# Squares in the diagonal blocks of a graph-attention layer's second pass, and an even pace for its finished rows

## The chip, the cores and the metric

The kernel runs on one NeuronCore of a Trainium2 chip. Its engines work in parallel, each through its own instructions in order: TensorE (PE; its weight loads are listed as PEld), VectorE (DVE), ScalarE (ACT), GpSimd (POOL) and SyncE (SP), which here only issues DMA transfers. On-chip data lies in SBUF and, for matmul results, in PSUM. The metric is the device time of one execution in microseconds (us).

## The reference

The input is x, 4096 x 512, and a sparse 0/1 matrix adj, 4096 x 4096. There are two layers; the change is in the first.

```
# layer 0
h = relu(layernorm(x))
node_att = softmax(h @ node_w, axis=0)
g = h @ edge_w
e = where(adj > 0, g @ g.T, -9e15)
edge_att = softmax(e, axis=1)
x = x + (adj * node_att * edge_att) @ (h @ weight) + bias
# layer 1: attention of 8 heads on the new x
h = relu(layernorm(x))
d = (h @ W.T + b) as (4096, 8, 64)
e = leaky_relu(src(d)[n] + trg(d)[m], 0.01) + adj
x = x + softmax(e) @ d
```

The score matrix g @ g.T is symmetric. All is computed in 32-bit floats.

## The kernel before

Rows are handled in 32 tiles of P = 128, and in 8 blocks of BL = 512 (TB = 4 tiles).

*First pass over the scores.* The blocks (i, j) with j >= i are computed on TensorE, written to `e_d` in HBM, and used for the row maxima. Only the upper half of the scores is stored; in a diagonal block, tile t stores the columns from its own start on.

*Second pass* (lines 364 to 486, from 700 to 1601 us). The outer loop runs over the blocks b of 512 output rows, the inner one over the tiles m of 128 neighbours: 256 steps (b, m). A step needs the scores of its 128 neighbours against the block's 512 rows, with neighbours in the partitions. It subtracts the row maxima (L441) and adds the mask (`mk`, L435; the sum is L442), takes the exponential on ACT (`ex`, L444), multiplies by adj (`at`, L450), adds `ex` to a sum on POOL (`racc`, L460), and multiplies `at` with the tile's rows of `sup` = h @ weight on TensorE into four PSUM tiles `po` (L480). Each 32-bit matmul shows as two records.

Where the scores come from depends on m. For tiles above the block (m // TB < b) they are loaded as they are (`et`, L396). For tiles below it (m // TB > b) the stored scores lie the other way round. They are then loaded in squares of S = 32 that stand at their transposed places (`squares`, L402 to L411: 16 DMAs for a group of four tiles into one buffer `eb`), and DVE, whose transpose turns each square of 32 x 32 in itself, turns them into a PSUM tile `pt` (L421). In the diagonal block (m // TB == b) the group's four row tiles are loaded into one `eb` (L392); for its tile i the first i of four column parts are missing, and TensorE transposes them from the tiles before (L427), i = 1, 2 and 3, six transposes of 128 x 128 in a block.

*The order of the work* is written out by hand. The loop at L652 to L669 calls the stages of several steps in turn: `load` of the step 8 ahead, `squares` of that 9 ahead, `turn` 3 ahead, `exps` 2, `masks` 3, `weigh` (L450, L460) 1 ahead, then `gather` (L480) of the step itself. Every engine and every DMA queue runs its instructions in this order. The loads of the second pass go through SP's queue; buffers come free when DVE has used them (11 for `a`, the tile of adj, 9 for `et`, 4 for `eb`, 3 for `at`).

*Finishing rows.* At a block's last step ACT copies its four `po` tiles to SBUF. During the next block, after `weigh`, the loop calls `finish` (L490) once for each of the four row tiles: DVE scales by the node attention and adds x (L499), and POOL issues a DMA to `x1` (L500). This happens at steps m = 2, 3, 4, 5 while b < 3, and at 2, 4, 6, 8 from b = 3 on.

*The path to layer 1.* Row tiles in `SQ` (L511) get their layer norm at once: `finish` adds bn_stats (L505), `layernorm` (L514) follows from m = 10 on, and the normalised rows are written to `h_d` as squares (SP, L532). Rows outside `SQ`, those of the first and the last block, are normalised later. After the second pass the loop `tail` (L615 to L648, 1601 to 1717 us) takes one row tile a step: `fetch` (L550) loads it; `stats` and `norm` normalise it if it is not in `SQ`; `turn_h` (L574) transposes it, on DVE from squares if it is in `SQ` (L577), otherwise on TensorE with a copy on ACT (L583, L585); `linear` (L587, L591) multiplies by W. Layer 1's attention follows from 1720 us on.

Of the kernel before, what the change touches and what calls it, by code (L numbers as in the profile page):

```python
# [15 lines left out]
P = 128  # L16
# [12 lines left out]
def kernel(  # L29
# [15 lines left out]
    nc = tc.nc  # L45
# [6 lines left out]
    BL = 512  # L52
    NB = N // BL
    TB = BL // P
# [3 lines left out]
    ident = const.tile([P, P], FP, name="ident")  # L58
# [17 lines left out]
    S = 32  # L76
    e_d = dram.tile([N, N + 2 * S], FP, name="e_d")[:, 0:N]
# [23 lines left out]
    with tc.tile_pool(name="w0", bufs=1) as wp, tc.tile_pool(name="a0", bufs=2) as ap_, tc.tile_pool(  # L101
# [32 lines left out]
        def stats(t):  # L134
            st = sp.tile([P, 6], FP, name="st")
            nc.vector.bn_stats(st, xts[t])
            mvs[t] = sp.tile([P, 2], FP, name="mv")
            nc.vector.bn_aggr(mvs[t], st)
            sds[t] = sp.tile([P, 1], FP, name="sd")
            nc.scalar.activation(sds[t], mvs[t][:, 1:2], AF.Sqrt, bias=eps)  # L140

        def norm(t):
            rs = sp.tile([P, 1], FP, name="rs")
            nc.vector.reciprocal(rs, sds.pop(t))
            mr = sp.tile([P, 1], FP, name="mr")
            nc.vector.scalar_tensor_tensor(mr, mvs.pop(t)[:, 0:1], -1.0, rs, op0=ALU.mult, op1=ALU.mult)
            hs[t] = sp.tile([P, F], FP, name="h", bufs=5)
            if t < T0:
                nc.scalar.activation(hs[t], xts[t], AF.Relu, bias=mr, scale=rs)
            else:  # L150
                nc.scalar.activation(squares_of(hs[t]), columns_of(xts[t]), AF.Relu, bias=mr, scale=rs)
# [24 lines left out]
        def turn(t):  # L176
            b, j = divmod(t, TB)
            if j == 0:
                hts[b] = ap_.tile([P, KC, BL], FP, name="h_t")
            if t >= T0:  # L180
                nc.vector.transpose(
                    hts[b][:, :, j * P:(j + 1) * P].rearrange("p k (a q) -> p k a q", q=S),
                    hqs.pop(t).rearrange("p (a k q) -> p k a q", k=KC, q=S))
                return
            h = hs.pop(t)
            pt = pp.tile([P, KC, P], FP, name="pt")
            for k in range(KC):
                nc.tensor.transpose(pt[:, k, :], h[:, k * P:(k + 1) * P], ident)
            nc.vector.tensor_copy(hts[b][:, :, j * P:(j + 1) * P], pt)
            logit(t, h)  # L190
# [25 lines left out]
        def step(t):  # L216
            if t < NT:
                upto(fetch, t + 10 if t >= T0 else t + 7)
                upto(norm, t + 4)
                upto(send, t + 4)  # L220
                turn(t)
                upto(pull, t + 2)
                upto(stats, t + 5)
# [47 lines left out]
    def maxima(i, acc, psum, pool):  # L271

        mx = pool.tile([P, TB], FP, name="mx")
        nc.vector.tensor_reduce(mx, rm[:, i * TB:(i + 1) * TB, i:NB], AX.X, ALU.max)
        pc = psum.tile([P, TB, P], FP, name="pt")
        for j in range(TB):
            nc.tensor.transpose(pc[:, j, :], acc[:, j * P:(j + 1) * P], ident)
        cm = pool.tile([P, TB], FP, name="cm")
        nc.vector.tensor_reduce(cm, pc, AX.X, ALU.max)
        nc.vector.tensor_tensor(mx, mx, cm, ALU.max)  # L280
        yield
        pm = psum.tile([P, BL], FP, name="pt")
        nc.tensor.transpose(pm[:TB, 0:P], mx, ident)
        ms = pool.tile([TB, P], FP, name="ms")
        nc.vector.tensor_copy(ms, pm[:TB, 0:P])
        nc.gpsimd.dma_start(mx_d[i], ms)


    with tc.tile_pool(name="mx", bufs=1) as mxp, tc.tile_pool(name="b_a", bufs=6) as adjp, tc.tile_pool(
# [6 lines left out]
        loaded, masks = {}, {}  # L296
# [52 lines left out]
        for n in range(-6, len(items)):  # L349
# [3 lines left out]
            if n >= 0:  # L353
                i, j, t = items[n]
# [9 lines left out]
    with tc.tile_pool(name="c_a", bufs=11) as adjp, tc.tile_pool(name="c_b", bufs=4) as ebp, tc.tile_pool(  # L364
# [10 lines left out]
        src, pts, aj, mks, ex, at = {}, {}, {}, {}, {}, {}  # L375

        def rows_of(m):
            return slice(m * P, (m + 1) * P)
# [23 lines left out]
        def squares(b, m):  # L402
            cols = slice(b * BL, (b + 1) * BL)
            if m // TB > b and m % TB == 0:
                eb = ebp.tile([P, TB, BL], FP, name="eb")
                sq = e_d[cols, m * P:m * P + BL].rearrange("(a p) (i c q) -> i c p a q", p=S, q=S, i=TB)
                for i in range(TB):
                    for c in range(P // S):
                        nc.sync.dma_start(eb[c * S:(c + 1) * S, i, :].rearrange("p (a q) -> p a q", q=S), sq[i, c])
                for i in range(TB):  # L410
                    src[b, m + i] = eb  # L411

        def turn(b, m):

            i = m % TB
            eb = src[b, m]
            pt = p_t.tile([P, BL], FP, name="pt")
            pts[b, m] = pt
            parts = []
            if m // TB > b:  # L420
                nc.vector.transpose(pt, eb[:, i, :])  # L421
                src[b, m] = [(slice(0, BL), pt)]
                return
            n = i if m // TB == b else 0
            if n > 0:
                for j in range(n):
                    nc.tensor.transpose(pt[:, j * P:(j + 1) * P], eb[:, j, i * P:(i + 1) * P], ident)  # L427
                parts.append((slice(0, n * P), pt))
            if n < TB:
                parts.append((slice(n * P, BL), eb[:, i, :] if m // TB == b else eb))  # L430
            src[b, m] = parts
# [56 lines left out]
        left, scale, norms = [], {}, iter(())  # L488

        def finish():  # L490

            t, acc, oc, rs, xt = left.pop(0)
            b, j = divmod(t, TB)
            if j == 0:
                sc = sp.tile([P, TB], FP, name="sc")
                nc.vector.reciprocal(sc, rs)
                nc.vector.tensor_tensor(sc, sc, na[:, b * TB:(b + 1) * TB], ALU.mult)
                scale[b] = sc
            nc.vector.scalar_tensor_tensor(oc, acc, scale[b][:, j:j + 1], xt, op0=ALU.mult, op1=ALU.add)  # L499
            nc.gpsimd.dma_start(x1[rows_of(t), :], oc)  # L500
            if t in SQ:
                if j == 0:
                    mv4[b] = sp.tile([P, TB, 2], FP, name="mv4", bufs=1), []
                st = sp.tile([P, 6], FP, name="st", bufs=4)
                nc.vector.bn_stats(st, oc)  # L505
                nc.vector.bn_aggr(mv4[b][0][:, j, :], st)
                mv4[b][1].append(oc)

        SQ = range(TB, (NB - 1) * TB)  # L511
        mv4 = {}

        def layernorm(b):  # L514
# [35 lines left out]
        def fetch(t):  # L550
            xl[t] = etp.tile([P, BL], FP, name="et")
            nc.sync.dma_start(xl[t], h_d[t] if t in SQ else x1[rows_of(t), :])

        def stats(t):
            if t in SQ:
                return
# [7 lines left out]
        def norm(t):  # L564
            if t in SQ:
                return
# [7 lines left out]
        def turn_h(t):  # L574
            if t in SQ:
                hts[t] = wkp.tile([P, BL], FP, name="d")
                nc.vector.transpose(hts[t].rearrange("p (k a q) -> p k a q", k=KC, q=S),  # L577
                                    xl.pop(t).rearrange("p (a k q) -> p k a q", k=KC, q=S))
                return
            h = hs.pop(t)  # L580
            pt = p_t.tile([P, BL], FP, name="pt")
            for k in range(KC):
                nc.tensor.transpose(pt[:, k * P:(k + 1) * P], h[:, k * P:(k + 1) * P], ident)  # L583
            hts[t] = wkp.tile([P, BL], FP, name="d")
            nc.scalar.copy(hts[t], pt)  # L585
# [27 lines left out]
        end = len(steps)  # L613
# [35 lines left out]

        stages = ((load, 8), (squares, 9), (turn, 3), (exps, 2), (masks, 3), (weigh, 1), (gather, 0))  # L652
        for s in range(-9, end):
            for f, ahead in stages:
                if 0 <= s + ahead < end:
                    f(*steps[s + ahead])
                if f is weigh:
                    b, m = divmod(s, NT)
                    if left and m > 1 and (m % 2 == 0 or b < 3):
                        finish()  # L660
                    if m == 10 and b - 1 in mv4:
                        norms = layernorm(b - 1)
                    if m >= 10:
                        next(norms, None)
                    tail(s - end)
                    if s == 3:
                        ending = maxima(NB - 1, acc_z, p_t, sp)
                    if s in (3, 4):
                        next(ending, None)  # L669
# [10 lines left out]
        pt = p_t.tile([P, BL], FP, name="pt")  # L680
# [53 lines left out]
    with tc.tile_pool(name="p", bufs=2) as prp, tc.tile_pool(name="rl", bufs=2) as rlp, tc.tile_pool(  # L734
# [322 lines left out]
        stages = ((load, 4), (exps, 1), (weigh, 1), (factors, 2), (logs, 0), (scale, 2), (gather, 0))  # L1057
# [48 lines left out]
```

## Time and profile before

| | |
|---|---|
| median of 3 runs | 2953.14 us (2951.71 to 2954.64) |
| the profiled execution: its time, its span | 2952.01 us, 2949.9 us |
| TensorE busy over the span | 2895.0 us, 98% |
| DVE, ACT, POOL busy | 2535.0, 1318.9, 1421.7 us |
| second pass, first to last matmul of L480 | 705.6 to 1601.3 us |
| tail, first matmul of L591 to its end | 1604.1 to 1717.3 us |
| mean of one transpose: TensorE 128 x 128 (L427, 48 of them), DVE 128 x 512 (L421, 112) | 282 ns, 720 ns |

The span runs from the first instruction to the last; the execution's time also holds what lies around it, 2.1 us here. Engine times are busy times. A matmul's record is longer than its share of TensorE, as the next one starts before it ends, so distances between starts tell how long a step lasts. A group's row gives source line, engine, operation, the tiles written and read, their sizes and the count; then the busy time and the mean of one, and the idle time before it with what ended it. In a row of the timeline the start and the length in us come first, and in brackets stands how long the engine was idle before, and what released it.

### The profile page before, as it was taken

To read this page: it belongs to the slowest core of one execution; us is meant where nothing else is said; L and a number is where in the kernel's file an instruction comes from. 1 tells how busy PE (TensorE), PEld (TensorE's weight loads), DVE (VectorE), ACT (ScalarE), POOL (GpSimd) and SP (SyncE) were. 2 spreads that over 40 slices of the span, in tenths; PEclk is the share of its full clock that TensorE was granted. 3 is DMA by queue.
4 is the path that set the end of the run, shared out by engine and by line. 5 is a ranking of instruction groups with operands and counts; after the bars stand their busy time and mean duration, and the time that the engine had idled before them with its cause. 6 is when DMAs were issued, how large, how long until landed. Compare 5 with 4: busy or idle time off the path is not lost.

```text
span 2949.9 us, 42840 instructions
## 1 busy us (share of the span) xinstructions
PE 2895.0 (98%) x15051; PEld 1152.0 (39%) x15051; DVE 2535.0 (86%) x3584; ACT 1318.9 (45%) x1822; POOL 1421.7 (48%) x1075
## 2 busy tenths in 40 slices
PE   8999999999999999999999989999999999999998
PEld 4444444444444444444444423333233223232223
DVE  5535777778888998998996789999999999999998
ACT  2211111111121221222222068888777777777776
POOL 3401111113544444444444766676767676766675
PEclk9999999999999999999999989999999999999999
DMA  5525666667875766756644269898989898989796
GB/s 182 175 75 199 223 220 224 226 218 192 202 178 162 174 166 185 187 161 179 198 160 135 61 173 237 232 229 237 234 241 232 238 231 237 235 237 233 208 226 168
DMA packets 488616, 583.47 MB, mean 198 GB/s; under 512 B 265464, under 2 KB 315672, under 8 KB 488400
## 3 DMA queue, kind: packets, MB, share of 16 engines
q1 hardware_dynamic: 431920, 406.70, 45.2%
q0 software_dynamic: 54464, 170.10, 26.1%
q10 hardware_dynamic: 2016, 3.93, 0.4%
q8 instruction: 118, 1.93, 0.3%
q14 instruction: 98, 0.80, 0.1%
HBM read 415.76 MB, written 72.55 MB: 166 GB/s over the span
## 4 chain that ended last, share of the span: by engine, by line
PE 74%; DVE 12%; ACT 7%; issue 4%; DMA 3%; POOL 0%; SPq 0%; DVEq 0%; ACTq 0%; POOLq 0%
PE po L480 29%; PE pe L331 15%; PE pv L885 14%; DVE pr L854 9%; PE dn L890 4%; PE po L591 4%; PE ps L196 3%; ACT e L822 3%; PE pe L203 3%; DMA acc<-pr 1%; ACT rl L840 1%; ACT ex L812 1%; DVE pr L851 1%; DMA e<-in_adj_t_dram 0%; PE pt L938 0%
## 5 line engine op out<-in xcount | busy, mean ns | idle before, releaser
L885 PE MATMUL pv<-pr,sup 128*32 128x512 f32 x8192 | 1024.0, 595 | 13.2 <-POOL d_m L1050 5.4
L480 PE MATMUL po<-sup,at 128*128 128x512 f32 x2048 | 887.0, 594 | 3.5 <-DVE at L450 3.5
L863 POOL TENSOR_TENSOR acc<-acc,pr 128x1024 f32<-128x1024 f32 x240 | 583.7, 2432 | 328.6 <-DVE pr L854 326.7
L854 DVE SCALAR_TENSOR_TENSOR pr<-z,g_m,ex 128x1024 f32<-128x1024 f32 x512 | 631.5, 1275 | 4.7 <-ACT ex L812 4.5
L480 PEld LDWEIGHTS po<-sup,at 128*128 128x128 f32 x2048 | 387.0, 190 | 483.1 <-issue 445.7
L460 POOL TENSOR_TENSOR racc<-racc,ex 128x512 f32<-128x512 f32 x240 | 365.8, 1524 | 381.7 <-ACT ex L444 380.2
L885 PEld LDWEIGHTS pv<-pr,sup 128*32 128x32 f32 x8192 | 301.9, 110 | 604.6 <-issue 503.4
L444 ACT ACTIVATE ex<-d 128x512 f32<-128x512 f32 x256 | 160.5, 630 | 624.5 <-DVE d L442 611.6
L331 PE MATMUL pe<-he_t,he_t 128*128 128x512 f32 x896 | 386.4, 592 | 0.0
L812 ACT ACTIVATE ex<-e 128x1024 f32<-128x1024 f32 x256 | 263.5, 1029 | 241.4 <-DVE pr L854 241.3
L890 PE MATMUL dn<-pr,d_m 128*2 128x512 f32 x1984 | 347.6, 592 | 0.0
L854 DVE SCALAR_TENSOR_TENSOR pr<-z,g_m,e 128x1024 f32<-128x1024 f32 x256 | 328.4, 1283 | 0.2 <-ACT e L822 0.2
L851 DVE SCALAR_TENSOR_TENSOR pr<-rl,ngd_m,ex 128x1024 f32<-128x1024 f32 x224 | 285.7, 1275 | 12.5 <-ACT ex L812 12.2
L822 ACT ACTIVATE e<-e,ld_m 128x1024 f32<-128x1024 f32 x256 | 291.3, 1138 | 0.6 <-DMA e<-in_adj_t_dram 0.6
L840 ACT ACTIVATE rl<-z,ngd_m,d_m 128x1024 f32<-128x1024 f32 x224 | 275.6, 1230 | 0.0
L335 POOL DMA_DIRECT2D e_d<-es x144 | 78.9, 548 | 364.3 <-ACT es L334 358.8
L450 DVE TENSOR_TENSOR at<-ex,a 128x512 f32<-128x512 f32 x256 | 189.6, 741 | 73.7 <-ACT ex L444 50.8
L331 PEld LDWEIGHTS pe<-he_t,he_t 128*128 128x128 f32 x896 | 169.2, 190 | 210.1 <-issue 190.0
L334 ACT COPY es<-pe 128x512 f32<-128x512 f32 (+2 forms) x144 | 79.3, 551 | 377.0 <-PE pe L331 377.0
L442 DVE TENSOR_TENSOR d<-pt,mk 128x512 f32<-128x512 f32 x256 | 177.0, 691 | 8.8
L336 DVE CUSTOM_DVE_ANT_0 mk<-pe,mk 128x512 f32<-128x512 f32 (+2 forms) x144 | 93.0, 646 | 99.1 <-ACT es L334 99.0
L869 POOL DMA_DIRECT2D acc<-pr x160 | 150.0, 937 | 1.2 <-DMA acc<-pr 0.5
(186 smaller groups left out, 2534.7 us busy)
## 6 DMA issues: line engine op xcount, KB each, us to landing
e<-in_adj_t_dram SPq DMA_DIRECT2D x256, 512.0 KB, 5.6
acc<-pr POOLq DMA_DIRECT2D x176, 512.0 KB, 5.6
a<-in_adj_t_dram SPq DMA_DIRECT2D x256, 256.0 KB, 3.6
ar<-in_adj_dram SPq DMA_DIRECT2D x120, 256.0 KB, 3.0
e_d<-es POOLq DMA_DIRECT2D x120, 256.0 KB, 3.1
eb<-e_d SPq DMA_DIRECT2D x456, 64.0 KB, 2.8
ac<-in_adj_t_dram SPq DMA_DIRECT2D x112, 256.0 KB, 3.6
et<-e_d SPq DMA_DIRECT2D x112, 256.0 KB, 3.7
```

The costliest lines, as they stand in the source:

```text
L331: nc.tensor.matmul(pe[:, :w], he_t[i][:, k, (t % TB) * P:(t % TB + 1) * P], he_t[j][:, k, BL - w:], start=(k == 0), stop=(k == KC - 1))
L450: nc.vector.tensor_tensor(w, e, aj.pop((b, m)), ALU.mult)
L460: nc.gpsimd.tensor_tensor(racc, racc, e, ALU.add)
L480: nc.tensor.matmul(po[j], w[:, j * P:(j + 1) * P], sup[:, m, :], start=(m == 0), stop=last)
L812: nc.scalar.activation(x_, ra.pop((i, m)), AF.Exp)
L822: nc.scalar.activation(x_, ra[i, m], AF.Exp, bias=ld_m[:, h // HG, m:m + 1])
L840: nc.scalar.activation(r, zs_[i, 0], AF.Relu, bias=ngd_m[:, h // HG, m:m + 1], scale=d_m[:, h, m:m + 1])
L851: nc.vector.scalar_tensor_tensor(w, rl.pop((i, m)), ngd_m[:, h // HG, m:m + 1], x_, op0=ALU.subtract, op1=ALU.mult)
L854: nc.vector.scalar_tensor_tensor(w, zs_[i, k], g_m[:, h + k, m:m + 1], e3.pop((i, m)) if k == 3 else x_, op0=ALU.max, op1=ALU.mult)
L863: nc.gpsimd.tensor_tensor(acc[i, 3], acc[i, 3], w, ALU.add)
L885: nc.tensor.matmul(v[c][q][r * D + c0:r * D + c0 + Q, :], va[:, m, g * HG + k, c0:c0 + Q], pr[i, m, k][:, q * BL:(q + 1) * BL], start=(m = ...
L890: nc.tensor.matmul(dn[r * Q:r * Q + w.shape[1], :], w, src[:, q * BL:(q + 1) * BL], **fl)
```

## The change

Four edits, all in the second pass and its path to layer 1:

- In the diagonal blocks, the parts that TensorE transposed are loaded as squares too: four DMAs for each of the tiles i = 1, 2, 3, into the part of `eb` that was empty, and one DVE transpose of i x 128 columns per tile in place of i transposes on TensorE.
- `squares` is called for the step 8 ahead, after `load` of the same step, and no longer for 9 ahead; the loop begins at -8.
- `SQ` begins at 0: the first block's rows are normalised during block 1 and go to layer 1 as squares.
- `finish` is called at m = 2, 4, 6, 8 in all blocks.

```diff
--- before.py
+++ after.py
@@ -409,6 +409,12 @@
                         nc.sync.dma_start(eb[c * S:(c + 1) * S, i, :].rearrange("p (a q) -> p a q", q=S), sq[i, c])
                 for i in range(TB):
                     src[b, m + i] = eb
+            if m // TB == b and m % TB > 0:
+                i = m % TB
+                sq = e_d[b * BL:b * BL + i * P, m * P:(m + 1) * P].rearrange("(a p) (c q) -> c p a q", p=S, q=S)
+                for c in range(P // S):
+                    nc.sync.dma_start(
+                        src[b, m][c * S:(c + 1) * S, i, 0:i * P].rearrange("p (a q) -> p a q", q=S), sq[c])
 
         def turn(b, m):
 
@@ -417,14 +423,9 @@
             pt = p_t.tile([P, BL], FP, name="pt")
             pts[b, m] = pt
             parts = []
-            if m // TB > b:
-                nc.vector.transpose(pt, eb[:, i, :])
-                src[b, m] = [(slice(0, BL), pt)]
-                return
-            n = i if m // TB == b else 0
+            n = TB if m // TB > b else i if m // TB == b else 0
             if n > 0:
-                for j in range(n):
-                    nc.tensor.transpose(pt[:, j * P:(j + 1) * P], eb[:, j, i * P:(i + 1) * P], ident)
+                nc.vector.transpose(pt[:, 0:n * P], eb[:, i, 0:n * P])
                 parts.append((slice(0, n * P), pt))
             if n < TB:
                 parts.append((slice(n * P, BL), eb[:, i, :] if m // TB == b else eb))
@@ -508,7 +509,7 @@
 
 
 
-        SQ = range(TB, (NB - 1) * TB)
+        SQ = range((NB - 1) * TB)
         mv4 = {}
 
         def layernorm(b):
@@ -649,14 +650,14 @@
 
 
 
-        stages = ((load, 8), (squares, 9), (turn, 3), (exps, 2), (masks, 3), (weigh, 1), (gather, 0))
-        for s in range(-9, end):
+        stages = ((load, 8), (squares, 8), (turn, 3), (exps, 2), (masks, 3), (weigh, 1), (gather, 0))
+        for s in range(-8, end):
             for f, ahead in stages:
                 if 0 <= s + ahead < end:
                     f(*steps[s + ahead])
                 if f is weigh:
                     b, m = divmod(s, NT)
-                    if left and m > 1 and (m % 2 == 0 or b < 3):
+                    if left and m > 1 and m % 2 == 0:
                         finish()
                     if m == 10 and b - 1 in mv4:
                         norms = layernorm(b - 1)
```

## The prediction

> **What bounds the kernel now.** I read the page first, then the busy time by stage, then the groups by form, then the timeline where a step of the second pass is longer than its neighbours. The change lies between 700 and 1720 us, so only that stretch matters. Busy time of the engines in five of its stretches (blocks 0 to 3, and the linear part of layer 1 that I call the tail); the columns after the window are its length, then PE, PEld, DVE, ACT and POOL busy, the clock, and the DMA share and rate:
>
> ```profile
> 705.60:819.10 113.50, 113.50 (x270) 50.86 (x271) 99.55 (x169) 21.91 (x35) 52.23 (x42) 0.98 0.86 191
> 819.10:930.50 111.40, 111.40 (x272) 50.03 (x271) 96.84 (x161) 22.27 (x36) 49.87 (x36) 1.00 0.68 169
> 930.50:1044.00 113.50, 111.98 (x272) 50.10 (x271) 100.88 (x167) 27.98 (x43) 47.50 (x36) 1.00 0.71 181
> 1044.00:1155.40 111.40, 111.40 (x272) 50.03 (x271) 99.58 (x163) 27.97 (x43) 50.07 (x36) 1.00 0.67 175
> ...
> 1601.30:1717.30 116.00, 114.15 (x293) 51.88 (x291) 79.97 (x142) 10.28 (x19) 79.95 (x65) 1.00 0.23 71
> ```
>
> TensorE fills every block. A step's eight matmul records of L480 follow each other every 0.43 us, so a bare step is 3.43 us, and 26 or 27 of the 32 steps of blocks 3 to 7 have just that length. DVE is close behind with 97 to 101 of 111 us. What is longer than 3.43 us has three causes. First, the transposes of the diagonal blocks (PE alone, in block 3: start, length, what):
>
> ```profile
> 1081.84 0.38 PE L427 MATMUL pt<-ident,eb 128*128 128x128 f32 x2
> 1082.05 3.60 PE L480 MATMUL po<-sup,at 128*128 128x512 f32 x8
> 1085.49 0.49 PE L427 MATMUL pt<-ident,eb 128*128 128x128 f32 x3
> 1085.82 4.46 PE L480 MATMUL po<-sup,at 128*128 128x512 f32 x10
> ```
>
> Two transposes hold the next matmul back by 0.21 us, three by 0.33: 0.11 each, though one record lasts 0.27. One block has 1+2+3 of them, 0.66 us; its steps read 3.54, 3.65 and 3.76. Second, in block 2 TensorE waits for `at` (steps of 4.12, 5.03 and 3.86 us, 2.05 us too long beside the 0.66). The timeline there, everything that DVE and POOL do in one such step:
>
> ```profile
> 946.60 0.75 DVE L499 SCALAR_TENSOR_TENSOR oc<-oc,sc,xt 128x512 f32<-128x512 f32 x1
> 947.38 0.69 DVE L505 BATCH_NORM_STATS2 st<-oc 128x6 f32<-128x512 f32 x1
> 947.64 0.55 POOL L500 DMA_DIRECT2D x<-oc  x1 [3.19 <-DVE oc L499]
> 948.11 0.18 DVE L506 BATCH_NORM_AGGREGATE mv<-st 128x2 f32<-128x6 f32 x1
> 948.21 1.85 DVE L441 TENSOR_TENSOR pt<-et,mb 128x512 f32<-128x512 f32 x1
> 948.21 1.28 POOL L460 TENSOR_TENSOR racc<-racc,ex 128x512 f32<-128x512 f32 x1
> ...
> 951.77 3.70 PE L480 MATMUL po<-sup,at 128*128 128x512 f32 x8 [0.41 <-DVE at L450]
> ```
>
> Finishing a row costs DVE 1.60 us, and its DMA holds POOL so that the sum on POOL starts together with the subtraction from SBUF, which takes 1.85 in place of 0.69. Four such steps in a row are more than TensorE's 3.43. Third, two starts: the pass's first step (5.58 us, half clock), and the tail:
>
> ```profile
> 1598.84 3.33 DVE L499 SCALAR_TENSOR_TENSOR oc<-po,sc,xt 128x512 f32<-128x512 f32 x4 [0.59 <-PE po L480]
> 1601.21 1.04 PE L583 MATMUL pt<-ident,at 128*128 128x128 f32 x8
> 1603.49 1.05 ACT L585 COPY d<-pt 128x512 f32<-128x512 f32 x2
> 1604.10 3.70 PE L591 MATMUL po<-eb,d 128*128 128x512 f32 x8 [1.85 <-ACT d L585]
> ```
>
> The tail's first matmul waits for two transposed tiles to come through TensorE and ACT; its first two steps take 3.97 and 3.87 us against 3.43 later, because each also transposes a tile.
>
> **What the Trainium skill says.** "TensorE: Matmul & The Clock Gate", Part 4: PE-mode transpose, has about 275 ns for a 128x128 transpose in a kernel; the record agrees (272), but only 107 ns of it is in the way here, and that is the price I use. "VectorE: DVE Perf Modes", The three transpose paths: VectorE transposes 32x32 blocks only, which is why the squares must be placed by DMA; its 311 ns for a bf16 128x128 I don't use, as the trace has 720 ns for 128x512 in f32. "DMA: Bandwidth & Descriptors", Specifications, wants transfers of 512 B or more; squares move 128 B rows, and the trace shows what that costs: 64 KB land every 0.5 us in a run of them. "TensorE: Matmul & The Clock Gate", Part 1: after an idle window of about 3.4 us the array runs at half clock until such a window was busy; the trace agrees at 705.6, with matmul starts some 0.85 us apart for 4 us before they come at 0.43.
>
> **The change, part by part.**
>
> *Diagonal blocks on TensorE.* 48 transposes go. Block 0's six ran before its first matmul, so they gain nothing. Blocks 1 to 7: 7 x 0.66 = 4.6 us, as long as DVE keeps up.
>
> *Diagonal blocks on DVE.* Three transposes per block, of 128, 256 and 384 columns. The trace has only 512 columns (720 ns, the next start after 0.63). The subtraction from PSUM shows how length scales on DVE: 294, 428, 545 and 669 ns. On that slope starts are about 0.22, 0.36 and 0.50 us apart: 1.1 us per block. Bounds: strictly by columns 0.95, each as long as a full one 1.9. I measure the cover by DVE's lead: the time from the end of `at` (L450) to the first matmul of its step. It grows by 0.56 us per step in the lower blocks and is full at 5.9. A block costs lead 0.66 + 1.1 = 1.8 us. Blocks 4 to 7 have 3.0 or more at these steps, so nothing is lost, and DVE's idle steps at the block's end (over 4 us) refill it. Block 3 has 1.99 us at its tightest such step: 0.2 stays. If that cover is gone, each missing microsecond is a microsecond of TensorE.
>
> *Twelve DMAs per block on SP, before the squares and loads behind them.* An issue takes about 0.53 us, fewer descriptors 0.35 to 0.45: 5 to 6 us more per block. Blocks 2 to 7 leave SP 40 us idle or more. In block 0 SP is busy 3.0 to 3.3 of 3.43 us in a step. There the load `a` of step 5, issued at 707.6 now, goes out at about 712.4 and lands near 715.7; DVE wants it at 714.5, and at about 715.6 when its own transposes have come first. Just covered. Later squares come about 5 us later than now and are wanted about as much later; SP needs 11.1 to 11.6 us for a group of four steps and TensorE 13.7, so it catches up. The squares for steps 1 to 3 follow right behind the second `a` (landed at 698.0) and are small; I put them at 699, 701 and 703 us, before DVE asks for them.
>
> *Start of the pass.* Transposes 1 and 2 stand on DVE before the first `at`, and DVE is without a gap from 701 us on: 0.22 + 0.36 = 0.6 later. Part of it passes at half clock anyway. I take 0.5 us lost; bounds 0 and, if a square is late, 2.5.
>
> *Squares one step later (8, not 9).* On SP's queue this only swaps a group of squares with one `a`; nothing waits for it. Zero.
>
> *Rows finished in every second step.* Block 2 then has block 3's pattern, which has leads of 2.57, 3.39, 1.78, 2.60, 1.01, 1.82, 0.33 us at steps 4 to 10 and no stall. Its own transposes fall on steps 7 to 9, so take 1.1 and 0.1 from the 0.33: a stall of up to 0.9, of which some vanishes because a transpose runs while POOL adds and the collision passes meanwhile. I take 0.6 of the 2.05 us remaining: 1.45 gained (0.85 to 2.05).
>
> *Block 0's rows as squares.* In block 1 DVE adds four times 0.87 us (statistics), and 0.33 for the scales; ACT adds four `hh` of 0.80, a root and two table loads of 1.28. SP adds 16 writes of h_d behind waits for `hh`; the loads queued behind them are eight steps ahead. Block 1's lead now is 3.30 us at step 10 (1.62 at step 7, growing by 0.56). After: 3.30 - 0.66 - 1.1 - 4 x 0.87 = -1.9. But now three subtractions collide with POOL there for 2.8 us together, and with finishing in every second step, a full transpose first, most of these fall away. Stall 0 to 1.9, I take 0.3.
>
> *The tail.* Four tiles lose statistics, root, scales, Relu, transposes on TensorE and ACT's copy; one DVE transpose each (0.70) replaces them. The first stands behind the last finished row (1602.17): 1602.87, matmul at 1602.95 in place of 1604.10, 1.15 us. The two steps lose 0.54 and 0.44. Together 2.1 us, hidden by nothing.
>
> **Sum.** Block 0 -0.5; block 1 0.66 - 0.3 = 0.4; block 2 0.66 + 1.45 = 2.1; blocks 3 to 7 5 x 0.66 = 3.3; tail 2.1. Together 7.4 us less. What follows the tail is untouched and moves with it. The profiled execution took 2952.0 us (span 2949.9), so 2944.6; it lay 1.1 below the median of the runs, 2953.14, so 2945.8 there. 0.2% is 5.9 us, about what a measurement of this kernel can tell from none.
>
> **Rivals.** *DVE takes it back* in blocks 1 to 3: stalls at the bounds (1.9, 1.2, and 0.5 in block 3) and a start worth 1.5: 7.4 - 1.6 - 0.6 - 0.5 - 1.0 = 3.7 us, 2949.4. For it: leads of 0.1 to 0.3 us at steps 10 and 13. Against: block 3 runs with them unstalled. *SP is late, slower than before*: if the start's stretched issues (one took 2.5 us) come on top, step 5's `a` lands 6 us after DVE asks; TensorE idles over 3.4 us and pays a second half-clock start (2.15 us as at the first), and in block 1, with 28 more DMAs at 0.5 us, another 2 us. 10.2 - 7.4: 2956. It decides from a lateness of about 5 us on. Against: the estimated lateness is 0. *No stall at all*, collisions all absorbed, start free: 7.4 + 0.3 + 0.6 + 0.5 = 8.8, 2944.3. *The transposes don't limit* (steps of blocks 3 to 7 stay over 3.43 because DVE sets them): then 3.3 of the 7.4 fall away, 2949.0; its chance is counted with DVE's.
>
> **How the numbers follow.** Forecast 0.60, no stall 0.10, DVE 0.23, SP 0.07. The forecast's own range is 2944.5 to 2947.5, and a little of it lies within 0.2%: faster 0.67, same 0.28, slower 0.05. For 8 in 10 I leave out SP and the outer parts of DVE's case (start and blocks all at their bounds) and of the no-stall case: 2943.2 to 2950.8.
>
> **What would show it.** Steps of 3.43 us at the diagonals of blocks 3 to 7; block 2 near 111.3 us; block 1 near 111.0; three stream transposes per diagonal of about 0.3, 0.45 and 0.6 us; the tail's first matmul about 1.6 us after the last of L480. Waits of TensorE for `at` in blocks 1 and 2, or of DVE for `eb` or `a` in the first 30 us, would make it wrong.

## The result and the profile after

The changed kernel takes 2944.12 us (median of 9 runs, 2942.85 to 2948.66) against 2954.44 us for the kernel before in the same comparison (9 runs, 2951.42 to 2960.86). The ratio is 0.9974 with a 95% interval of 0.9966 to 0.9982: 0.26% faster, about 7.7 us (5.3 to 10.0 inside the interval; the two medians by themselves lie 10.3 us apart). The forecast was 7.4 us and 2945.8 us.

The profiled execution took 2943.79 us, its span is 2941.9 us in place of 2949.9. Not all of these 8.0 us are the change's. The stretch before the second pass, which no edit touches, ended 1.5 us earlier, and what follows the tail was 0.3 us longer. I therefore measure from the start of the first pass's last matmul (L331) to the end of the tail (0.43 us after the start of its last matmul): 1017.53 us before, 1010.78 after, 6.75 us less. Kernels profiled again below repeat this stretch to 0.2 us, while the stretch before it ended anywhere from 697.5 to 704.3 us.

The busy time by stage in the profile after, with the columns and the stretches of the table for the kernel before (blocks 0 to 3, then the tail):

```profile
704.60:818.10 113.50, 113.50 (x269) 50.90 (x270) 100.15 (x170) 21.92 (x35) 48.25 (x42) 0.98 0.86 189
818.10:928.90 110.80, 110.80 (x266) 49.64 (x265) 98.92 (x174) 27.96 (x43) 47.09 (x36) 1.00 0.77 190
928.90:1040.50 111.60, 111.01 (x265) 49.53 (x264) 100.38 (x170) 27.96 (x43) 47.30 (x36) 1.00 0.73 185
1040.50:1152.00 111.50, 111.04 (x265) 49.54 (x264) 101.20 (x166) 27.97 (x43) 47.01 (x36) 1.00 0.69 179
1595.20:1709.00 113.80, 112.34 (x277) 50.49 (x276) 80.02 (x139) 6.35 (x12) 80.51 (x65) 1.00 0.26 76
```

Six matmul records fewer per block on PE, block 1 without a gap, and in blocks 2 and 3 PE is busy for 0.6 and 0.5 us less than the window: a short wait each. Where the 6.75 us went, from the starts of the matmuls of L481 (L480 before) and L592 (L591):

| stretch | before | after | change | forecast |
|---|---|---|---|---|
| last matmul of L331 to the first of the pass | 5.98 | 6.50 | +0.52 | +0.5 (with block 0) |
| block 0 | 113.46 | 113.55 | +0.09 | |
| block 1 | 111.42 | 110.76 | -0.66 | -0.4 |
| block 2 | 113.47 | 111.62 | -1.85 | -2.1 |
| block 3 | 111.42 | 111.49 | +0.07 | -0.66 |
| blocks 4 to 7 | 445.84 | 443.06 | -2.78 | -2.6 |
| gap before the tail, tail | 115.94 | 113.79 | -2.15 | -2.1 |

In block 3 TensorE's transposes are gone from the row, but a wait stands in their place (TensorE alone):

```profile
1072.70 12.61 PE L481 MATMUL po<-sup,at 128*128 128x512 f32 x29
1085.77 4.56 PE L481 MATMUL po<-sup,at 128*128 128x512 f32 x10 [0.46 <-DVE at L451]
```

The tail's start in the profile after, to set beside the four lines of before:

```profile
1592.69 3.33 DVE L500 SCALAR_TENSOR_TENSOR oc<-po,sc,xt 128x512 f32<-128x512 f32 x4 [0.59 <-PE po L481]
...
1595.93 1.29 DVE L578 STREAM_TRANSPOSE d<-et 128x512 f32<-128x512 f32 x2
...
1596.69 1.55 PE L592 MATMUL po<-eb,d 128*128 128x512 f32 x3 [1.46 <-DVE d L578]
```

The last row finished ends at 1596.0, DVE turns two tiles one after the other behind it, and TensorE begins 0.1 us after the first is done. The two tiles that TensorE transposed and ACT copied no longer stand in between.

### The profile page after: what moved, and what is told of

It is laid out like the page before. It is cut to its first block, busy times and chain, and to the rows that moved or that the text cites. A ratio compares the mean times of both kernels' runs of the same rounds, so it can differ in the third digit from the quotient of the medians.

```text
span 2941.9 us, 42890 instructions
## 1 busy us (share of the span) xinstructions
PE 2885.6 (98%) x14987; PEld 1144.6 (39%) x14987; DVE 2536.9 (86%) x3606; ACT 1317.9 (45%) x1817; POOL 1410.4 (48%) x1075
## 3 DMA queue, kind: packets, MB, share of 16 engines
q8 instruction: 117, 1.92, 0.3%
## 4 chain that ended last, share of the span: by engine, by line
PE 73%; DVE 11%; ACT 7%; issue 4%; DMA 3%; POOL 1%; SPq 0%; DVEq 0%; ACTq 0%; POOLq 0%
PE po L481 28%; PE pe L331 15%; PE pv L886 14%; DVE pr L855 9%; PE dn L891 4%; PE po L592 4%; ACT e L823 3%; PE pe L203 3%; PE ps L196 3%; DMA acc<-pr 2%; ACT rl L841 1%; ACT ex L813 1%; DVE pr L852 1%; DMA xb_d<-xb 1%; DMA eb<-e_d 0%
## 5 line engine op out<-in xcount | busy, mean ns | idle before, releaser
L481 PE MATMUL po<-sup,at 128*128 128x512 f32 x2048 | 884.1, 594 | 7.2 <-DMA eb<-e_d 6.1
L481 PEld LDWEIGHTS po<-sup,at 128*128 128x128 f32 x2048 | 389.4, 191 | 493.8 <-issue 452.4
L461 POOL TENSOR_TENSOR racc<-racc,ex 128x512 f32<-128x512 f32 x240 | 354.2, 1476 | 388.2 <-ACT ex L445 386.8
L331 PE MATMUL pe<-he_t,he_t 128*128 128x512 f32 x896 | 386.4, 592 | 0.0
L331 PEld LDWEIGHTS pe<-he_t,he_t 128*128 128x128 f32 x896 | 169.6, 190 | 209.8 <-issue 190.4
L451 DVE TENSOR_TENSOR at<-ex,a 128x512 f32<-128x512 f32 x256 | 187.3, 732 | 66.9 <-ACT ex L445 41.6
```

The costliest lines, as they stand in the source:

```text
L331: nc.tensor.matmul(pe[:, :w], he_t[i][:, k, (t % TB) * P:(t % TB + 1) * P], he_t[j][:, k, BL - w:], start=(k == 0), stop=(k == KC - 1))
L451: nc.vector.tensor_tensor(w, e, aj.pop((b, m)), ALU.mult)
L461: nc.gpsimd.tensor_tensor(racc, racc, e, ALU.add)
L481: nc.tensor.matmul(po[j], w[:, j * P:(j + 1) * P], sup[:, m, :], start=(m == 0), stop=last)
```

## The experiments

Each was timed in five rounds against the kernel before. One kernel measured against itself (the fourth) gives a ratio of 1.000 with an interval of 0.9992 to 1.0008, 2.4 us either way, so the parts of 0.5 to 3 us are told apart in the traces, by the stretch defined above (1010.78 us in the changed kernel) and by the blocks. In all profiles the first step of the pass starts with matmuls some 0.85 us apart in place of 0.43 (the half clock of the prediction), and its length varied from 5.2 to 6.5 us without any edit that explains it. This is the uncertainty in block 0.

### One edit undone at a time

```diff
-            if m // TB == b and m % TB > 0:
+            if m // TB == b and False:
...
-                nc.vector.transpose(pt[:, 0:n * P], eb[:, i, 0:n * P])
+                if m // TB > b:
+                    nc.vector.transpose(pt[:, 0:n * P], eb[:, i, 0:n * P])
+                else:
+                    for j in range(n):
+                        nc.tensor.transpose(pt[:, j * P:(j + 1) * P], eb[:, j, i * P:(i + 1) * P], ident)
```

> The changed kernel with one edit undone: the diagonal blocks' parts are transposed on TensorE again; pace, first block's rows and the squares' place stay. Theory (TensorE sets the step, a transpose costs it 0.11 us, and DVE transposes cost lead): blocks 1, 4, 5, 6 and 7 show steps of 3.54, 3.65 and 3.76 again, +0.66 us each; the stalls of 0.87 us in block 2 and 0.74 us in block 3 go, so these stay at about 111.4 us; the pass starts 0.5 us sooner. Sum +2.4 us against the changed kernel, about 5 us under the kernel before. Rival (DVE sets the steps, so TensorE's transposes were hidden): no longer steps anywhere, and the two stalls and the start come out 2 us faster than the changed kernel.

Measured: 1013.57 us, 2.79 us more than the changed kernel; ratio to the kernel before 0.9980 (0.9973 to 0.9987). Blocks 1 and 4 are 0.66 us longer and blocks 5, 6 and 7 0.69 to 0.71, with the old steps of 3.54, 3.65 and 3.76 us; blocks 2 and 3 take 111.42 us without a wait, and the pass starts after 5.97 us. The theory holds block by block: TensorE paid for its transposes, and DVE's transposes cost TensorE time only where DVE's lead was short. The sum is larger than the 2.4 us expected, 0.18 of it by the half-clock step, and the kernel is 4.0 us under the kernel before in this stretch, not 5.

```diff
-                    if left and m > 1 and m % 2 == 0:
+                    if left and m > 1 and (m % 2 == 0 or b < 3):
```

> The changed kernel with the old pace of finishing: every step from 2 to 5 in blocks 1 and 2. Theory (four finishes in a row, 1.6 us each and a collision with POOL's sum, drain DVE's lead): TensorE waits in block 1 for about 1.8 us and in block 2 for about 2.6 us in place of 0.87; 3.5 us slower than the changed kernel. Rival (only the total of DVE's work in the block counts): both blocks as in the changed kernel, within 0.5 us.

Measured: 1013.57 us, 2.79 more; ratio 0.9992 (0.9984 to 1.0000). Block 1 is 1.63 us longer, block 2 1.53, block 0 0.5 shorter by its half-clock step; 1.8, 1.7 and in all 3.5 us were expected. In block 1 (TensorE alone):

```profile
835.71 7.60 PE L481 MATMUL po<-sup,at 128*128 128x512 f32 x17
844.53 5.85 PE L481 MATMUL po<-sup,at 128*128 128x512 f32 x13 [1.22 <-DVE at L451]
```

The same work of DVE costs 3.2 us more, the two blocks together, when four finishes come in a row. The rival that only totals count is out.

```diff
-        SQ = range((NB - 1) * TB)
+        SQ = range(TB, (NB - 1) * TB)
```

> The changed kernel with the first block's rows outside the early layer norm again. Theory: the tail's first matmul comes 1.2 us later and its first two steps are 0.5 and 0.4 us longer; block 1 is as in the changed kernel, since it has no stall there. 2.1 us slower than the changed kernel. Rival (the early norm of block 0 costs block 1 what the tail gains): block 1 gets shorter by up to 1 us and the sum is near 0.

Measured: 1012.79 us, 2.01 more; ratio 0.9986 (0.9979 to 0.9994). The gap before the tail is 2.89 us and the tail 113.05, together 2.15 us more; block 1 stays at 110.76. The early norm of block 0's rows, which runs during block 1, costs block 1 nothing.

The fourth kernel is the kernel before, with no edit.

> The kernel before, unchanged, against itself, for what the measurement can tell and for a second profile. Expected ratio 1.000, interval within 0.001 of it. The stretch before the second pass, which no edit touches, ended 1.5 us earlier in the profile of the changed kernel; if that is chance, this profile's end of that stretch lies anywhere between 698 and 700 us.

Measured: ratio 1.000 (0.9992 to 1.0008). The stretch is 1017.35 us (1017.53 in the first profile), the first pass's end 698.86 us (699.62). So the 6.75 us are the change's, and the 1.5 us ahead of it lie well within what this stretch varies by from profile to profile (697.5 to 704.3 us).

### The two waits that were larger than forecast

DVE's lead over TensorE in block 3 (from the end of `at` to the first matmul of its step) is 0.24, 0.26, 0.42 and 0.06 us at steps 10 to 13; before it was 0.33, 1.36, 1.92 and 1.99. With the 0.74 us that TensorE waits, DVE has lost 2.7 us by step 13. TensorE's missing transposes and 1.1 us on DVE explain 1.8 us of that. The timeline of DVE and POOL shows the rest, first the step of the diagonal's first tile in the kernel before:

```profile
1077.99 0.69 DVE L441 TENSOR_TENSOR pt<-eb,mb 128x512 f32<-128x512 f32 x1
1078.00 1.80 POOL L460 TENSOR_TENSOR racc<-racc,ex 128x512 f32<-128x512 f32 x1 [2.16 <-ACT ex L444]
```

Then the same tile, and the third one (`mb` subtracted from its 256 columns), in the profile after:

```profile
1074.52 0.32 DVE L428 STREAM_TRANSPOSE pt<-eb 128x128 f32<-128x128 f32 x1
1074.54 1.26 POOL L461 TENSOR_TENSOR racc<-racc,ex 128x512 f32<-128x512 f32 x1 [2.16 <-ACT ex L445]
1074.75 1.60 DVE L442 TENSOR_TENSOR pt<-eb,mb 128x512 f32<-128x512 f32 x1
...
1082.50 1.26 POOL L461 TENSOR_TENSOR racc<-racc,ex 128x512 f32<-128x512 f32 x1 [3.29 <-ACT ex L445]
1082.53 1.53 DVE L442 TENSOR_TENSOR pt<-eb,mb 128x256 f32<-128x256 f32 x1
```

The subtraction for the diagonal's first tile reads SBUF alone. The next tile's transpose of 0.32 us now stands in front of it; POOL's sum starts 0.02 us after the transpose, and the subtraction ends 0.55 us after the sum has ended: 1.60 us instead of the 0.69 it took before, when it started first and the sum was stretched to 1.80. The second collision comes from the norm: a table load on ACT at 1080.44 delays `ex`, so POOL's sum meets the third tile's subtraction, which took 0.43 us before. Three kernels separate the two.

```diff
-        stages = ((load, 8), (squares, 8), (turn, 3), (exps, 2), (masks, 3), (weigh, 1), (gather, 0))
+        stages = ((load, 8), (squares, 8), (exps, 2), (turn, 3), (masks, 3), (weigh, 1), (gather, 0))
```

> The changed kernel with two stages swapped in the loop: the exponentials' subtraction of step s+2 is issued ahead of the transpose of step s+3. Nothing else changes, DVE's work is the same. Theory A (the transpose in front of a subtraction from SBUF lets POOL's sum take the port first, and the subtraction then lasts 1.5 to 1.6 us in place of 0.7): the 512-column subtraction of a diagonal block falls from a mean of 1471 ns to about 1100 or less, the stalls of 0.87 us in block 2 and 0.74 us in block 3 go or shrink to 0.2; 1.4 us faster than the changed kernel. Theory B (the stalls come from the sheer 1.1 us of transposes): both stalls stay as they are.

Measured: 1011.18 us, 0.40 more; ratio 0.9978 (0.9970 to 0.9986). Block 3's wait is gone (110.76 us), but block 2's grew (112.01), and block 1 got one of 0.65 us (111.41). The groups of the subtraction from `eb` by width, first the changed kernel, then this one (after the count: busy, mean ns):

```profile
L442 DVE TENSOR_TENSOR pt<-eb,mb 128x512 f32<-128x512 f32 x8 | 11.8, 1471 | 0.0
L442 DVE TENSOR_TENSOR pt<-eb,mb 128x384 f32<-128x384 f32 x8 | 7.7, 957 | 0.3
L442 DVE TENSOR_TENSOR pt<-eb,mb 128x128 f32<-128x128 f32 x8 | 3.4, 430 | 0.3
```

```profile
L442 DVE TENSOR_TENSOR pt<-eb,mb 128x384 f32<-128x384 f32 x8 | 9.9, 1237 | 0.3
L442 DVE TENSOR_TENSOR pt<-eb,mb 128x512 f32<-128x512 f32 x8 | 7.7, 960 | 0.0
L442 DVE TENSOR_TENSOR pt<-eb,mb 128x128 f32<-128x128 f32 x8 | 5.9, 739 | 0.3
```

With the subtraction in front, the 512 columns of the first tile take 0.69 us in blocks 2 to 6; the 384, 256 (mean 718 to 885 ns) and 128 columns of the others now meet more of the sum. Theory A is right for the first tile, but its forecast of 1.4 us less failed, as it is wrong as a rule for all: behind a transpose, the other tiles' subtractions let part of the sum pass.

```diff
-                    if m == 10 and b - 1 in mv4:
+                    if m == (18 if b == 3 else 10) and b - 1 in mv4:
```

> The changed kernel with the early layer norm in block 3 begun at step 18 and not at 10, away from the diagonal's steps 12 to 15. Theory B (in block 3 the norm's table loads delay POOL's sum into the subtraction, 1.5 us at 1082.5, and its scales cost DVE 0.4): block 3's stall of 0.74 us goes, block 2's 0.87 us stays. Theory A alone (the transposes in front, whatever the norm does): block 3 keeps at least half of its stall.

Measured: 1010.81 us, as much as the changed kernel, because the half-clock step was 0.8 us longer this time; ratio 0.9975 (0.9966 to 0.9985). Block 3 takes 110.76 us, its wait is gone, and block 2 keeps its own. In block 3 the third tile's subtraction no longer meets the start of POOL's sum:

```profile
1083.36 0.65 DVE L442 TENSOR_TENSOR pt<-eb,mb 128x256 f32<-128x256 f32 x1
```

The first tile's subtraction still takes 1.60 us, and 0.70 us of lead is left at step 13 (0.33 us of it are the norm's scales on DVE, which moved away too). So in block 3 the first tile's collision alone stays within the lead, and "Theory A alone" fails. Whether the norm's collision alone does, and what holds up block 2, where no norm falls on these steps, the next kernel decides.

```diff
+            b, m = divmod(max(s, 0) + 2, NT)
+            order = (0, 1, 3, 2, 4, 5, 6) if m == b * TB and s >= 0 else range(7)
-            for f, ahead in stages:
+            for f, ahead in (stages[i] for i in order):
```

> The changed kernel with the swap of subtraction and transpose in one step per block only: that of the diagonal's first tile (blocks 1 to 7), where the subtraction reads SBUF alone and no row was finished just before. Theory (a transpose in front of it lets POOL's sum in, which costs DVE 0.9 us of lead; elsewhere, and above all after a finished row, the transpose in front is right): this subtraction takes 0.7 us in place of 1.6, the stalls of 0.87 us in block 2 and 0.74 us in block 3 go or fall below 0.2, block 1 stays without one; 1.4 to 1.6 us faster than the changed kernel. Rival (the collision only moves to the mask or the product that follows): the stalls stay within 0.3 us of what they are.

Measured: 1009.42 us, 1.36 less than the first profile of the changed kernel and 1.47 less than the second; ratio 0.9965 (0.9952 to 0.9977). Blocks 1 and 3 take 110.76 us, block 2 110.84 (a step of 3.51 is left). The step in block 3:

```profile
1075.20 0.69 DVE L442 TENSOR_TENSOR pt<-eb,mb 128x512 f32<-128x512 f32 x1
1075.21 1.80 POOL L461 TENSOR_TENSOR racc<-racc,ex 128x512 f32<-128x512 f32 x1 [2.16 <-ACT ex L445]
...
1076.53 0.32 DVE L428 STREAM_TRANSPOSE pt<-eb 128x128 f32<-128x128 f32 x1
```

The subtraction is not held up, and POOL's sum takes 1.80 us in place of 1.26; POOL, busy for 47 us of a block, has the time. The mask behind the transpose has 0.54 us in place of 0.42, so little of the collision moves on. The rival is out. In block 3 the norm's collision is still there (1.53 us), and 0.28 us of lead is left at step 13: either cause alone stays within the lead, and only both together stall TensorE. In blocks 1 and 7 POOL's sum starts 0.5 us ahead of this subtraction, which stays slow (1.76 us); the swap pays in blocks 2 and 3 alone, the two that had a wait.

### The start and the loads on SP

```diff
-            if m // TB == b and m % TB > 0:
+            if m // TB == b and m % TB > 0 and b > 0:
...
-                nc.vector.transpose(pt[:, 0:n * P], eb[:, i, 0:n * P])
+                if b > 0 or m // TB > b:
+                    nc.vector.transpose(pt[:, 0:n * P], eb[:, i, 0:n * P])
+                else:
+                    for j in range(n):
+                        nc.tensor.transpose(pt[:, j * P:(j + 1) * P], eb[:, j, i * P:(i + 1) * P], ident)
```

> The changed kernel with block 0's diagonal alone transposed on TensorE as before, so 12 DMAs and three DVE transposes fewer at the start of the pass. Theory: the first matmul comes 0.53 us sooner after the first pass's last one (5.97 in place of 6.50 us), DVE never waits for a load of adj in block 0 (now 2.4 and 0.9 us at steps 13 and 17), the rest is unchanged; 0.5 us faster. Rival (the start is set by the loads' landing): start as now.

Measured: 1010.09 us, 0.69 less; ratio 0.9974 (0.9965 to 0.9984). The first matmul comes after 5.97 us, and DVE's lead stays full at 5.90 us through block 0, where the changed kernel's fell to 3.96. What it fell by is a wait for the load of adj of step 17, while TensorE was at step 13 of block 0 (profile after):

```profile
753.88 0.43 DVE L436 TENSOR_SCALAR mk<-a 128x512 f32<-128x512 f32 x1 [2.41 <-DMA a<-in_adj_t_dram]
```

```diff
                 for c in range(P // S):
-                    nc.sync.dma_start(
-                        src[b, m][c * S:(c + 1) * S, i, 0:i * P].rearrange("p (a q) -> p a q", q=S), sq[c])
+                    to = src[b, m][c * S:(c + 1) * S, i, 0:i * P].rearrange("p (a q) -> p a q", q=S)
+                    h = i * (P // S) // 2
+                    for part in (slice(0, h), slice(h, 2 * h)) if b == 0 else (slice(0, 2 * h),):
+                        nc.sync.dma_start(to[:, part, :], sq[c][:, part, :])
```

> The changed kernel with each of block 0's twelve new square loads split into two halves: the same bytes, 12 more issues on SP, some 4.5 us, ahead of the loads of adj of steps 5 and on. Theory (SP's lateness is covered just so far: DVE waited 0.3 us for step 5's load): DVE waits about 4.5 us there, TensorE's lead of 2.8 us at that step is used up, and block 0 gets 2 to 3 us longer. Rival (loads have slack that hides this): block 0 within 0.3 us of 113.55.

Measured: 1014.03 us, 3.25 more; ratio 0.9987 (0.9980 to 0.9993). Block 0 is 2.37 us longer, and the pass starts another 0.89 us later, since DVE's transposes now wait for their squares. DVE, then TensorE:

```profile
718.40 0.43 DVE L438 TENSOR_SCALAR mk<-a 128x512 f32<-128x512 f32 x1 [2.65 <-DMA a<-in_adj_t_dram]
```

```profile
707.59 10.02 PE L483 MATMUL po<-sup,at 128*128 128x512 f32 x21
...
719.49 3.70 PE L483 MATMUL po<-sup,at 128*128 128x512 f32 x8 [1.44 <-DVE at L453]
```

The wait for the load itself is shorter than expected (2.65, not 4.5), because DVE had already waited 3.3 us for late squares. The point stands: the cover at the start was nearly used up, and twelve more issues turn into 3.25 us.

### Both together

The kernel with block 0's diagonal on TensorE and the swap for the first tile has the two diffs above.

> The same with block 0's diagonal on TensorE besides: the start 0.53 us sooner as well, so 2.1 us less than the changed kernel from the first pass's last matmul to the tail's end, about 1008.6 us in place of 1010.8 and of 1017.5 in the kernel before; 0.3% under the kernel before if both gains add up.

Measured: 1009.33 us; ratio 0.9969 (0.9958 to 0.9980). The pass starts 0.53 us sooner and the two waits are gone, but the half-clock step was 6.23 us, 0.5 more than in the swap alone, so the sum of 1008.6 is not seen in this one profile. The half-clock step does not seem to take the 0.53 us back as a rule: over the 13 profiles it averages 5.71 us with the first diagonal on TensorE (five of them) and 5.69 with it on DVE (eight). The two ratios, 0.9965 and 0.9969, don't tell whether the first diagonal on TensorE gains anything beside the swap.

> The changed kernel, unchanged, beside the two: 1010.8 us from the first pass's last matmul to the tail's end, stalls of 0.87 us in block 2 and 0.74 us in block 3 as before; ratio to the kernel before between 0.997 and 0.998. The stretches ahead of the second pass and after the tail, which no edit touches, differ by up to several us between profiles of one kernel.

Measured beside these two: 1010.89 us, block 2 111.63, block 3 111.51; ratio 0.9973 (0.9964 to 0.9981). The swap is the better version by its trace, 1.4 us; in the times its interval overlaps that of the changed kernel.

## Why the prediction was right

*Sum.* 7.4 us were forecast; the traces show 6.75 and the times about 7.7. The forecast case came true in its main parts: TensorE sets the step, its transposes cost 0.66 us a block, and the tail and the start moved as put. That the sum is so close is in part luck: block 3 lost 0.73 us and block 2 0.26 against the forecast, block 1 won 0.30 and blocks 4 to 7 0.14. The median of 2944.12 us even lies 0.4 us below the forecast's own range, next to the 2944.3 of the rival without any stall; the traces rule that rival out, since there are two stalls.

*Its own signs.* Of what it named in advance, block 1 (110.76 us for about 111.0), the three transposes and the tail's first matmul came as said. Block 2 took 111.62 us in place of 111.3, the steps at the diagonal of block 3 were not all 3.43, and two of the signs that it is wrong did show: TensorE waits for `at` in block 2, and DVE waits 0.27 us for `a` 9 us into the pass. So the mechanism was right for blocks 1 and 4 to 7 and for the tail, and incomplete for blocks 2 and 3.

*Diagonal blocks on TensorE.* Right. 0.66 us each in blocks 1 and 4, and 0.69 to 0.71 in blocks 5 to 7, where a former wait of 0.04 us at step 13 went too (in the second profile of the changed kernel it is back in two of the three); the kernel with that edit undone has them again.

*Diagonal blocks on DVE.* The transposes last 320, 454 and 586 ns, starts about 0.22, 0.37 and 0.50 us apart, as put. The conclusion "Block 3 has 1.99 us at its tightest such step: 0.2 stays" failed: 0.74 us of waiting. The missing term is not the transposes' length but what they do to the order of DVE and POOL: the first tile's subtraction went from 0.69 to 1.60 us, and with the norm's delay the third tile's from 0.43 to 1.53. With either of the two taken away, no wait is left in block 3. "VectorE: DVE Perf Modes" of the Trainium skill, Two Vector instructions with no wait between them, says that the second read interface of SBUF is shared with GpSimd; the durations here agree with such a conflict, though no run shows the interface itself.

*Rows in every second step.* The working took it that "a transpose runs while POOL adds and the collision passes meanwhile". That holds after a finished row (384 columns in block 1: 1.87 us before, 0.97 after) and is the other way round for the first tile. Block 2's wait was 0.87 us for the 0.6 taken, at the upper bound of 0.9 (the range of 0.85 to 2.05, and the rival, imply one of 1.2). That it met the bound is chance: the bound reckoned with no new collision, and with the first tile's taken away (the swap kernel) 0.08 us of wait is left. Block 1, for which 0.3 was taken, had none: its three old collisions, which added 3.3 us to what these subtractions take alone and not the 2.8 put, fell to 1.5. The errors of blocks 1, 2 and 3, -0.3, +0.3 and +0.7 us, all lie in this one kind of term, how long subtractions and POOL's sums hold each other up.

*Start.* 0.52 us later for 0.5. Step 5's load went out at 710.6 and landed at 713.7, within 0.5 us of the forecast's 712.4 and 715.7 less the 1.5 us by which this execution was early; DVE waited 0.27 us. "It catches up" was too hopeful: DVE waited 2.4 and 0.9 us while TensorE was at steps 13 and 17, hidden only by a lead of 5.9 us. The rival with SP late was near: twelve more issues would have cost 3.25 us.

*Tail.* 2.15 us for 2.1: 1.27 in the gap, 0.88 in the first steps. *Squares at 8:* no wait shows that points to it; it was not tried alone.

## What to carry to other kernels

When two engines are nearly as busy as each other (here 111 us of a block and 97 to 101), moving work from the slower to the faster pays only as long as the faster has lead at that very step. Read the lead step by step, from the end of the product to the start of the work that uses it, before pricing the move. The order of two instructions on DVE can be worth more than the shorter of them: here a subtraction of two SBUF operands that starts just before POOL's sum takes 0.69 us, and one that starts 0.2 us after it 1.60. Small gains in a kernel with jitter of some microseconds outside the edited part are better read from the edited stretch of the trace than from whole times.

## What was not expected of the hardware

The subtraction of 512 columns in SBUF on DVE and POOL's sum hold each other up, and which of them waits goes with a few nanoseconds. In 733 cases of the 13 profiles here the two start within 0.02 us of each other. In 442 of them the subtraction starts 11 to 20 ns ahead: it takes 0.69 to 0.70 us and the sum 1.79 to 1.81. In the other 291 it starts between 8 ns ahead and 7 ns behind: it takes 1.83 to 1.86 us, ending 0.57 us after the sum, and the sum 1.27 to 1.28. No start lies between the two groups. The first follow directly on a product (L451), the second on the statistics of a finished row, as in the step of block 2 shown with the prediction; no run separates the start from what stands in front of it. With a transpose of 0.32 us in front on DVE, POOL's sum is 0.2 us ahead, takes 1.26 us, and the subtraction 1.60.

The transposes from SBUF into PSUM were not stretched in any of these collisions (0.72 us for 512 columns beside POOL's sum or without it).
